# Sparse graph attention, layers 0 and 1: scores by accumulated transposes, one exponential per chunk, softmax sums as matmuls

## The chip, the cores and the metric

The kernel runs on one core of one Trainium2 chip. A core has TensorE (matmuls, with a weight load ahead of each), VectorE, ScalarE, GpSimd (called POOL in the profile, it issues the gathers here) and SyncE, which issues plain DMAs. Each takes its instructions in program order and waits on semaphores. The core also has 16 DMA engines. The metric is the device time of one execution in microseconds. Lower is better.

## The reference

Four graph layers follow one another on `x`, 8 batches of 2048 nodes of 128 features. One adjacency matrix, with about 16 neighbours per node, serves all. Layers 0 and 1 are attention with 8 heads of 16, restricted to neighbours, followed by a feed-forward network. Layers 2 and 3 are graph attention with one score per node pair.

```python
def layer01(adj_matrix, h, Wq, Wk, Wv, Wo, bo, ln1_g, ln1_b, W1, b1, W2, b2, ln2_g, ln2_b):
    Q, K, V = ((h @ w).reshape(B, N, NUM_HEADS, HEAD_DIM) for w in (Wq, Wk, Wv))
    scores = jnp.einsum('bnhd,bmhd->bhnm', Q, K) / jnp.sqrt(HEAD_DIM)
    scores = jnp.where((adj_matrix == 0)[None, None], -jnp.inf, scores)
    attn = jax.nn.softmax(scores, axis=-1)
    attn_out = jnp.einsum('bhnm,bmhd->bnhd', attn, V).reshape(B, N, OUT_DIM)
    x = _layer_norm(h + (attn_out @ Wo + bo), ln1_g, ln1_b)
    y = jax.nn.relu(x @ W1 + b1) @ W2 + b2
    return _layer_norm(x + y, ln2_g, ln2_b)

def layer23(x, adj, W, a_src, a_dst, ln_gamma, ln_beta):
    h = x @ W
    e = (h @ a_src)[:, :, None] + (h @ a_dst)[:, None, :]
    e = jnp.where(e >= 0, e, NEG_SLOPE * e)
    att = softmax(jnp.where(adj == 0, -jnp.inf, e))
    return _layer_norm(jnp.einsum('bij,bjd->bid', att, h) + x, ln_gamma, ln_beta)
```

## The kernel before

**Tiles and slots.** A start phase reads the adjacency matrix, makes a list of neighbours for every node and sorts the nodes by their number of neighbours. 16 tiles of 128 nodes follow, one node per partition. Tile t has `CAPS[t]` slots, from 30 down to 11; slot s of a tile holds the s-th neighbour of each of its 128 nodes. Unused slots get -1e30 in `lmask`, so their weight becomes 0. The first tile folds the neighbours beyond 28 of its 16 fullest nodes over all partitions (`folded`), with a query spread to match (`qf`) and a matrix `merge` that brings the parts together.

**Chunks.** In layers 0 and 1 a chunk is two slots (sometimes one), in layers 2 and 3 four. For each slot GpSimd issues an indirect DMA that gathers 128 rows of a table in DRAM: 2048 numbers per node in layers 0 and 1, keys and values of all 8 batches. There are six buffers `kv` for chunks; `fetch` (L1118) issues gathers up to four chunks ahead, as soon as a buffer's last reader is done.

**One attention chunk** (`attention_chunk`, L634) is a generator that the main loop steps on:

1. VectorE multiplies the keys in place by the query (L642, 2048 numbers per partition for two slots). The 128 products of a batch lie as 16 groups of 8 heads, so the sum within a head is a sum over the 16 groups.
2. VectorE folds the products, by halves and in place (L647): from 128 to 64 columns, and in chunks with `k // 2` even to 32 as well. TensorE adds up what is left with the identity matrix, 8 or 4 matmuls accumulating in the PSUM tile `pair` (L650).
3. ScalarE takes the exponential, one instruction per slot, since the mask is its bias per partition (L655), and writes `w` in SBUF.
4. Two chunks later VectorE multiplies the values by `w` in place (L661), and TensorE adds the slots up by transposing each of the 8 batches' 128 x 128 blocks into the accumulator `acc` (`add_up` and `turn_into`, L328), 8 transposes per slot.

After the last chunk of a tile `reciprocal_sums` (L461) adds the weights of all slots on VectorE in a tree (L469, L471), takes their min and max for a final test (L478, L479) and the reciprocal (L480). `scales` (L682) spreads it over the columns, turns it with TensorE and copies it out; `outputs` (L676) multiplies `acc` by it. Then a tail (`attention_tail`, two halves of four batches) computes projection, norms, feed-forward and the next layer's rows, mostly on TensorE and ScalarE.

**Order.** The schedule is written by hand. The loop in `layers` (L1189) goes over the chunks. For chunk i it does the second slot's add-up of chunk i-3, issues gathers, then step 1, a `slot()`, steps 2 and 3, a `slot()`, step 4 of chunk i-2 with its first slot's add-up, and a `slot()`. Each `slot()` steps on all running tails and threads by one stage, so that their instructions stand between those of the chunks on TensorE and ScalarE. At the end a flag says whether all sums were within `SUM_MIN` and `SUM_MAX`; if not, a general path (not taken here) computes everything again.

Of the kernel before, what the change touches and what calls it, by code (L numbers as in the profile page):

```python
# [8 lines left out]
F32 = mybir.dt.float32  # L9
F16 = mybir.dt.float16  # L10
BF16 = mybir.dt.bfloat16
# [38 lines left out]
SUM_MIN, SUM_MAX = 1e-25, 1e30  # L50
# [34 lines left out]
def sparse_path(ctx: ExitStack, tc: tile.TileContext, ins: dict, out: bass.AP, flag: bass.AP):  # L85
# [46 lines left out]
    )  # L132
    eps = const.tile([P, 1], F32, name="eps")
# [17 lines left out]
    lmask = const.tile([P, sum(CAPS)], F32, name="lmask")  # L151
# [309 lines left out]
    def reciprocal_sums(l, t, w, columns, folded):  # L461
# [3 lines left out]
        if l < 2:  # L465

            while n > 2:
                m = -(-n // 2)
                nc.vector.tensor_add(w[:, : n - m, :], w[:, : n - m, :], w[:, m:n, :])  # L469
                n = m  # L470
            nc.vector.tensor_add(sums, w[:, 0, :], w[:, 1, :])  # L471
        else:
            nc.vector.tensor_reduce(
                sums, w[:, :n, :].rearrange("p s c -> p c s"), axis=AX.X, op=ALU.add
            )
# [157 lines left out]

    def attention_chunk(l, c):  # L634
        box, t, k, ns = c["box"], c["t"], c["k"], c["ns"]
        if k == 0:
            box["acc"] = pacc.tile([P, NB, P], F32, tag="acc", name="acc")
            box["w"] = work.tile([P, max(CAPS), NB * NH], F32, tag="w", name="w")
        acc, w, q = box["acc"], box["w"], box["qf" if c["folded"] else "q"]
# [4 lines left out]
        width = D  # L644
        for _ in range(2 - k // 2 % 2):
            width //= 2
            nc.vector.tensor_add(kk[:, :, :, :width], kk[:, :, :, :width], kk[:, :, :, width : 2 * width])  # L647
        sc = pair[:, : ns * NB * NH].rearrange("p (s b h) -> p s b h", b=NB, h=NH)
        for j in range(0, width, NH):
            nc.tensor.matmul(  # L650
                sc, ident, kk[:, :, :, j : j + NH], start=j == 0, stop=j + NH == width
            )
        for i in range(ns):
            at = first[t] + k + i
            nc.scalar.activation(  # L655
                w[:, k + i, :], sc[:, i].rearrange("p b h -> p (b h)"), AF.Exp,
                bias=lmask[:, at : at + 1], scale=1.0,
            )
# [4 lines left out]
            w[:, k : k + ns, :].rearrange("p s (b h) -> p (s b) h", h=NH)[:, :, None, :]  # L663
# [3 lines left out]
        if c["folded"]:  # L667
            folded_sums(w[:, BASE:, :], box)
# [4 lines left out]
    def sums(l, t, box):  # L673
        box["r"] = reciprocal_sums(l, t, box["w"], NB * (NH if l < 2 else 1), box.get("folded"))
# [7 lines left out]
    def scales(l, box):  # L682

        box["scale"] = scale = work.tile([P, NB, P], F32, tag="oT", name="scale", bufs=1)
        if l < 2:
            r = box["r"].rearrange("p (b h) -> p b h", h=NH)
            nc.scalar.copy(
                scale.rearrange("p b (j h) -> p b j h", h=NH),
                r[:, :, None, :].to_broadcast([P, NB, HD, NH]),
# [127 lines left out]
    def gat_tail(l, t, box):  # L817
# [5 lines left out]
        else:  # L823
            n = work.tile([P, max(CAPS), NB * NH], F32, tag="w", name="n")
# [71 lines left out]
    def start():  # L896
# [54 lines left out]
        same = small.tile([P, NT, BINS], BF16, tag="same", name="same", bufs=1)  # L951
        more = small.tile([P, NT, BINS], BF16, tag="more", name="more", bufs=1)
# [26 lines left out]
        def neighbours(t):  # L979
            val = work.tile([P, max(CAPS), NB * NH], F32, tag="w", name="val")  # L980
# [207 lines left out]

    def layers():  # L1189
# [9 lines left out]
        for i in range(len(every) + 2):  # L1199
            c1, c, n1, n2 = (chunk(i + j) for j in range(-1, 3))  # L1200
            while added:
# [25 lines left out]
            if n1["l"] in (2, 3) and n1["folded"]:  # L1227
                go(n1)
            if c1["l"] in (2, 3) and c1["last"]:
# [8 lines left out]
            while weighed and len(weighed) > (2 if c["l"] in (0, 1) else 0):  # L1238
                c2 = weighed.pop(0)
                if c2["last"]:  # L1240
                    sums(c2["l"], c2["t"], c2["box"])
                    threads.append(scales(c2["l"], c2["box"]))
                go(c2, 2)
                added.append(c2)
# [536 lines left out]
```

## Time and profile before

| | us |
|---|---|
| median of 5 runs | 3145.77 (3118.6 to 3157.37) |
| the profiled execution | 3139.88, its span 3138.1 |
| first to last L642 (attention chunks) | from 170.7 to 2070.6 |
| layers 2 and 3 | from about 2080 to the end |

| group | count | busy us | mean ns |
|---|---|---|---|
| L642 VectorE, keys times query, 2048 per partition | 268 | 612.2 | 2284 |
| L328 TensorE, transposes into `acc` (all layers) | 8208 | 1089.4 | 287 |
| L650 TensorE, score matmuls, 128 columns | 3168 | 421.9 | 284 |
| L650 TensorE, the same, 64 columns | 176 | 21.3 | 272 |
| L503 ScalarE, 128 columns from PSUM | 512 | 146.5 | 377 |
| L496 ScalarE, 128 columns from PSUM | 512 | 181.4 | 367 |

A line of a group names the line of the kernel, the engine, the operation, output and inputs, their shapes and the count; then the busy time and the mean duration of one. Matmuls overlap, so the mean of one is longer than its share of the busy time: for L328 1089.4 us over 8208 is 133 ns. A matmul of fp32 numbers is two instructions, a transpose one. Behind a second bar stands the time that the engine sat idle just before the group, and who ended it.

### The profile page before, as it was taken

What the parts mean: (1) busy time and instruction counts of PE and PEld (TensorE: products, weight loads), DVE (VectorE), ACT (ScalarE), POOL (GpSimd) and SP (SyncE); (2) the same over time, 40 slices, a digit from 0 to 9 for tenths busy, and PEclk for the clock granted to TensorE, in tenths of its full rate; (3) what the DMA queues carried; (4) which work ended last, traced back from release to release, by engine and by line L of the source; (5) the groups of instructions that cost most, each with busy time, mean ns of one, the idle gap of its engine ahead of it and who ended that gap; (6) DMA issues with size and microseconds to landing.
All of it is one profiled execution on the core that took longest, in us unless ns stands there. A gap on an engine that the chain in (4) does not pass through costs nothing.

```text
span 3138.1 us, 52148 instructions
## 1 busy us (share of the span) xinstructions
PE 2575.6 (82%) x19258; PEld 2346.1 (75%) x19258; DVE 2748.6 (88%) x2960; ACT 1340.8 (43%) x4895; POOL 1787.9 (57%) x1296
## 2 busy tenths in 40 slices
PE   5766888888889996788898999996778888688786
PEld 4655777777888886677787888885677778577776
DVE  8898999999999997999999999985878876677886
ACT  3511344444445551243443545553445545144354
POOL 0266678588566534555456555544666654666662
PEclk8978999999999998999999999998888889888898
DMA  8688888898889867688888888866898987999994
GB/s 328 247 331 317 313 302 315 327 335 324 322 332 338 322 268 302 248 325 331 313 315 334 340 318 330 316 225 245 337 345 329 361 331 281 338 340 364 369 366 163
DMA packets 200692, 987.63 MB, mean 315 GB/s; under 512 B 31918, under 2 KB 33712, under 8 KB 128436
## 3 DMA queue, kind: packets, MB, share of 16 engines
q0 software_dynamic: 175024, 890.45, 76.0%
q1 hardware_dynamic: 20502, 75.52, 6.4%
q10 hardware_dynamic: 4904, 18.24, 1.5%
q8 instruction: 155, 2.54, 0.3%
q14 instruction: 107, 0.88, 0.1%
HBM read 937.16 MB, written 91.55 MB: 328 GB/s over the span
## 4 chain that ended last, share of the span: by engine, by line
PE 42%; DVE 28%; issue 11%; DMA 7%; ACT 6%; POOL 2%; another core or an unknown queue 1%; DVEq 0%; POOLq 0%; ACTq 0%
PE acc L328 17%; DVE kv L642 10%; DVE kv L661 9%; DMA kv<-table,lists 5%; PE pair L650 5%; DVE kv L647 4%; PE m L754 2%; PE m L733 2%; PE m L335 2%; PE m L328 2%; PE m L838 2%; PE m L550 2%; ACT n L846 2%; PE m L559 1%; DMA kv<-table,sorted_lists 1%
## 5 line engine op out<-in xcount | busy, mean ns | idle before, releaser
L321 POOL DMA_INDIRECT kv<-table,lists x955 | 1327.7, 1390 | 874.0 <-PE acc L328 550.5
L328 PE MATMUL acc<-ident,kv 128*128 128x128 f32 x8208 | 1089.4, 287 | 203.4 <-DVE kv L661 99.4
L328 PEld LDWEIGHTS acc<-ident,kv 128*128 128x128 f32 x8208 | 987.3, 149 | 303.3 <-issue 166.5
L642 DVE TENSOR_TENSOR kv<-kv,q 128x2048 f32<-128x2048 f32 (+1 forms) x282 | 629.3, 2231 | 51.6 <-DMA kv<-table,sorted_lists 18.5
L661 DVE TENSOR_TENSOR kv<-kv,w 128x2048 f32<-128x2048 f32 (+1 forms) x284 | 632.7, 2228 | 0.0
L650 PE MATMUL pair<-kv,ident 128*128 128x128 f32 (+1 forms) x3344 | 443.3, 283 | 151.1 <-DVE kv L647 64.9
L650 PEld LDWEIGHTS pair<-kv,ident 128*128 128x128 f32 x3344 | 410.8, 197 | 175.9 <-issue 102.4
L799 DVE TENSOR_TENSOR kv<-kv,pair 128x3584 f32<-128x3584 f32 (+1 forms) x150 | 540.1, 3601 | 2.2 <-PE acc L328 0.4
L655 ACT ACTIVATE w<-pair,lmask 128x64 f32<-128x64 f32 x554 | 144.8, 311 | 748.9 <-PE pair L650 720.2
L647 DVE TENSOR_TENSOR kv<-kv 128x1024 f32<-128x1024 f32 (+1 forms) x434 | 442.7, 1020 | 14.4
L496 ACT ACTIVATE n<-m,eps 128x128 f32<-128x128 f32 x512 | 181.4, 367 | 298.1 <-PE m L720 153.8
L321 POOL DMA_INDIRECT kv<-table,sorted_lists x153 | 182.7, 1194 | 142.8 <-PE acc L328 74.0
L846 ACT ACTIVATE n<-m,eps 128x128 f32<-128x128 f32 x256 | 90.7, 372 | 313.1 <-PE acc L328 133.8
L804 ACT ACTIVATE kv<-kv,ws 128x128 f32<-128x128 f32 x554 | 176.5, 402 | 92.8 <-DVE ws L793 51.3
L517 POOL DMA_INDIRECT table<-rows,perm x57 | 90.8, 1593 | 137.1 <-ACT score L570 39.9
L754 PE MATMUL m<-w_L_w,hT 128*128 128x128 f32 x1024 | 156.2, 275 | 0.0
L503 ACT ACTIVATE n<-m,rs 128x128 f32<-128x128 f32 x512 | 146.5, 377 | 1.1
L810 DVE TENSOR_TENSOR kv<-kv 128x1024 f32<-128x1024 f32 x75 | 91.5, 1221 | 62.1 <-ACT kv L804 62.0
L680 DVE TENSOR_TENSOR o<-acc,scale 128x512 f32<-128x512 f32 x128 | 82.7, 684 | 63.9 <-PE acc L328 33.2
L754 PEld LDWEIGHTS m<-w_L_w,hT 128*128 128x128 f32 x1024 | 134.9, 192 | 0.0
L733 PE MATMUL m<-n1T,w_L_gnn_W 128*128 128x512 f32 x256 | 131.5, 597 | 0.6 <-ACT q L608 0.6
L335 PE MATMUL m<-ident,n 128*128 128x128 f32 x640 | 110.2, 293 | 17.0 <-ACT n L854 8.0
(238 smaller groups left out, 3624.2 us busy)
## 6 DMA issues: line engine op xcount, KB each, us to landing
kept<-xT SPq DMA_DIRECT2D x48, 512.0 KB
xT<-kept SPq DMA_DIRECT2D x48, 512.0 KB
kv<-in_adj_dram SPq DMA_DIRECT2D x16, 1024.0 KB
table<-kv ACTq DMA_DIRECT2D x16, 1024.0 KB
kv<-table,lists POOLq DMA_INDIRECT x955
kv<-in_x_nodes_dram SPq DMA_DIRECT2D x16, 512.0 KB
kv<-table,sorted_lists POOLq DMA_INDIRECT x153
found<-cand POOLq DMA_DIRECT2D x16, 64.0 KB
```

Of the source, the lines that this page charges most:

```text
L321: nc.gpsimd.indirect_dma_start(out=dst, out_offset=None, in_=tables[l][:, :], in_offset=bass.IndirectOffsetOnAxis(ap=index, axis=0), bound ...
L328: nc.tensor.matmul(dst, src, ident, start=start, stop=True, is_transpose=True, skip_group_check=True)
L335: nc.tensor.transpose(pt[:, j * P : (j + 1) * P], src[:, j, :], ident)
L496: nc.scalar.activation(dst[:, i, :], z[:, i, :], AF.Square, bias=eps, scale=D**-0.5, accum_out=ss[:, i : i + 1],)
L642: nc.vector.tensor_mul(kk, kk, q[:, None].to_broadcast([P, ns, NB, D]))
L647: nc.vector.tensor_add(kk[:, :, :, :width], kk[:, :, :, :width], kk[:, :, :, width : 2 * width])
L650: nc.tensor.matmul(sc, ident, kk[:, :, :, j : j + NH], start=j == 0, stop=j + NH == width)
L661: nc.vector.tensor_mul(vv, vv, w[:, k : k + ns, :].rearrange("p s (b h) -> p (s b) h", h=NH)[:, :, None, :] .to_broadcast([P, ns * NB, HD, ...
L733: nc.tensor.matmul(ph, wt["1"][:, f * P : (f + 1) * P], n1T.rearrange("p b c -> p (b c)"), start=True, stop=True,)
L754: nc.tensor.matmul(y[:, j, :], hT[:, f, j, :], wt["2"][:, f, :], start=False, stop=f == 1, skip_group_check=True,)
L799: nc.vector.tensor_mul(hv[:, :, :nv, :], hv[:, :, :nv, :], wc[:, :, :nv, None].to_broadcast([P, ns, nv, D]))
L804: nc.scalar.mul(hv[:, i, b, :], hv[:, i, b, :], ws[:, i, b - nv : b - nv + 1])
```

## The change

Only layers 0 and 1 are touched. Gathers, the product of keys and query, the values' product, add-ups and tails stay.

- **Fold.** VectorE does one fold in every chunk (128 to 64 columns), and writes it to a new tile `hk`, ordered by group of heads j, then slot, batch and head.
- **Scores.** TensorE transposes the eight blocks `hk[:, j, :]`, adding them up in `pair[:m, :128]`. The scores now have slot, batch and head on the partitions, and the nodes along the columns. The mask can't be a bias any more: one bfloat16 matmul per slot adds it (`lmask` is now bfloat16). One exponential covers the chunk; it writes `eT`.
- **Turn back.** One chunk later TensorE transposes `eT` into `pair[:, 128:128 + m]`, and ScalarE copies that to `weights` in SBUF, which the values' product reads.
- **Sums.** After eight chunks, and after a tile's last chunk, matmuls of every `eT` with `fold_slots` (two identities of 64 on top of each other) add the weights up in PSUM. ScalarE copies the sum out, and after the last chunk takes its logarithm; `scales` uses exp(-log). The tree and the reciprocal are no longer run in layers 0 and 1; the min and max are. The bounds of the final test are narrower.
- **Order.** `scales` starts with the turn back of a tile's last chunk, some two chunks earlier. Every iteration of the main loop begins with the turn back of the chunk before.
- Tiles that shared the buffers of the old `w` get the new shape, and two tiles of the start phase use the buffers of `hk`.

```diff
-SUM_MIN, SUM_MAX = 1e-25, 1e30
+SUM_MIN, SUM_MAX = 1e-15, 1e15
...
+    fold_slots = const.tile([P, NB * NH], F32, name="fold_slots")
+    nc.vector.tensor_add(fold_slots, ident[:, : NB * NH], ident[:, NB * NH :])
...
-    lmask = const.tile([P, sum(CAPS)], F32, name="lmask")
+    lmask = const.tile([P, sum(CAPS)], BF16, name="lmask")
...
+    def block_sums(l, t, box, last):
+
+        terms = [(e, fold_slots[: e.shape[0], :]) for e, folded in box["exps"] if not folded]
+        if "partial" in box:
+            terms.append((ident, box["partial"]))
+        if last and t == 0:
+            terms += [(merge, box["wf"][:, i, :]) for i in range(FOLD)]
+        ps = misc()[:, : NB * NH]
+        for i, (a, b) in enumerate(terms):
+            nc.tensor.matmul(
+                ps, a, b, start=i == 0, stop=i + 1 == len(terms), skip_group_check=True
+            )
+        name = "sums" if last else "partial"
+        box[name] = small.tile([P, NB * NH], F32, tag=name, name=name)
+        nc.scalar.copy(box[name], ps)
+        box["exps"].clear()
+        if last:
+            box["r"] = small.tile([P, NB * NH], F32, tag="logs", name="logs", bufs=1)
+            nc.scalar.activation(box["r"], ps, AF.Ln)
+            threads.append(scales(l, box))
...
-        width = D
-        for _ in range(2 - k // 2 % 2):
-            width //= 2
-            nc.vector.tensor_add(kk[:, :, :, :width], kk[:, :, :, :width], kk[:, :, :, width : 2 * width])
-        sc = pair[:, : ns * NB * NH].rearrange("p (s b h) -> p s b h", b=NB, h=NH)
-        for j in range(0, width, NH):
+        m, at = ns * NB * NH, first[t] + k
+        hk = work.tile([P, NH, P], F32, tag="hk", name="hk")[:, :, :m]
+        kj = kk.rearrange("p s b (j h) -> p (s b) j h", h=NH)
+        nc.vector.tensor_add(
+            hk.rearrange("p j (c h) -> p c j h", h=NH), kj[:, :, :NH, :], kj[:, :, NH:, :]
+        )
+        sc = pair[:m, :P]
+        for j in range(NH):
+            turn_into(sc, hk[:, j, :], j == 0)
+        for i in range(ns):
             nc.tensor.matmul(
-                sc, ident, kk[:, :, :, j : j + NH], start=j == 0, stop=j + NH == width
-            )
-        for i in range(ns):
-            at = first[t] + k + i
-            nc.scalar.activation(
-                w[:, k + i, :], sc[:, i].rearrange("p b h -> p (b h)"), AF.Exp,
-                bias=lmask[:, at : at + 1], scale=1.0,
-            )
+                sc[i * NB * NH : (i + 1) * NB * NH, :],
+                lmask[:, at + i : at + i + 1].to_broadcast([P, NB * NH]), ident_bf,
+                start=False, stop=True, skip_group_check=True,
+            )
+        eT = box["eT"][:m, len(box["exps"]) % NH, :]
+        nc.scalar.activation(eT, sc, AF.Exp)
+        box["exps"].append((eT, c["folded"]))
+        yield
+        back = pair[:, P : P + m]
+        nc.tensor.matmul(
+            back, eT, ident[:m, :m], start=True, stop=True, is_transpose=True, skip_group_check=True
+        )
+        w = small.tile([P, P], F32, tag="weights", name="weights", bufs=3)[:, :m]
+        nc.scalar.copy(w, back)
...
+        if c["last"] or len(box["exps"]) == NH:
+            block_sums(l, t, box, c["last"])
         yield
...
-            nc.scalar.copy(
+            nc.scalar.activation(
                 scale.rearrange("p b (j h) -> p b j h", h=NH),
-                r[:, :, None, :].to_broadcast([P, NB, HD, NH]),
+                r[:, :, None, :].to_broadcast([P, NB, HD, NH]), AF.Exp, scale=-1.0,
             )
...
+            for c2 in weighed[-1:]:
+                go(c2)
             while added:
...
```

## The prediction

> **What bounds the kernel now.** I read the page's totals and slices first, to find the engine that is hardly ever idle in the attention layers, then the stages, the chain of waits in one of them, 10 us windows inside a tile, and the groups by shape.
>
> ```profile
> PE 2575.6 (82%) x19258; PEld 2346.1 (75%) x19258; DVE 2748.6 (88%) x2960; ACT 1340.8 (43%) x4895; POOL 1787.9 (57%) x1296
> ...
> DVE  8898999999999997999999999985878876677886
> ...
> DMA  8688888898889867688888888866898987999994
> ```
>
> Columns 3 to 26 are the two attention layers: VectorE shows 9 nearly throughout, DMA 8 and TensorE 6 to 9. The stages in numbers (span, TensorE, weight loads, VectorE, ScalarE, GpSimd, clock, DMA share, GB/s):
>
> ```profile
> 240.00:1045.00 805.00, 680.28 (x5256) 621.89 (x5255) 777.26 (x713) 342.22 (x1170) 562.96 (x328) 0.98 0.87 323
> 1250.00:2010.00 760.00, 670.90 (x5362) 618.72 (x5361) 733.94 (x544) 327.50 (x1241) 422.59 (x238) 0.98 0.84 316
> ```
>
> VectorE is idle for 28 us of 805 and 26 of 760. But TensorE has only 125 and 89 us to spare, and the DMA engines 13 to 16%. Two windows of 10 us inside one tile show that the three take turns:
>
> ```profile
> 1600.00:1610.00 10.00, 5.94 (x47) 5.31 (x48) 9.96 (x8) 2.00 (x6) 5.92 (x4) 1.00 1.02 427
> 1630.00:1640.00 10.00, 10.00 (x78) 8.87 (x77) 9.89 (x7) 6.15 (x21) 4.51 (x2) 1.00 0.72 261
> ```
>
> In the first no tail of an earlier tile runs: DMA is full, TensorE 60% busy. In the second a tail runs: TensorE never stops, DMA falls to 0.72. VectorE is full in both. The chain of waits of the first stage, by line, says who decides:
>
> ```profile
> by line: DVE kv L642 17.1%; DVE kv L661 16.0%; issue 9.7%; DMA kv<-table,lists 9.4%; PE acc L328 8.9%; DVE kv L647 7.5%; PE pair L650 6.5%; PE m L754 3.1%; PE m L733 3.1%; PE m L535 2.3%; DVE o L680 1.7%; PE m L335 1.7%; POOL kv L321 1.6%;
> ```
>
> Only 7.5% of the chain is the line that the change shortens. Summed by engine from its pieces, the chain is 47% VectorE and 31% TensorE here, 45% and 41% in layer 1. So VectorE is first, with TensorE and DMA close behind it.
>
> **VectorE: what goes.** The groups by shape:
>
> ```profile
> L661 DVE TENSOR_TENSOR kv<-kv,w 128x2048 f32<-128x2048 f32 x270 | 616.5, 2283 | 0.0
> L647 DVE TENSOR_TENSOR kv<-kv 128x1024 f32<-128x1024 f32 x270 | 330.5, 1224 | 8.8
> L647 DVE TENSOR_TENSOR kv<-kv 128x512 f32<-128x512 f32 x158 | 109.6, 694 | 5.4
> L655 ACT ACTIVATE w<-pair,lmask 128x64 f32<-128x64 f32 x554 | 144.8, 311 | 748.9 <-PE pair L650 720.2 <-issue 20.1 <-PE m L335 7.4
> ```
>
> There are 284 attention chunks, 270 of two slots and 14 of one. Of the 158 adds of 512 elements, 14 are first folds of one-slot chunks, so 144 are second folds; with six of 256 elements at some 0.42 us that is 144 x 0.694 + 2.5 = 102 us. The weight sums are L469 50.9 us (its sum over windows), L471 7.2 and the 64-wide reciprocal 17.7: 76 us. Together 178 us leave VectorE. The min and max of the sums stay. The first fold stays too, but it now writes `hk` in runs of 8 elements 128 apart. No row has such a write; L661 reads its weights in runs of 8 at 2.283 us, no more than L642's 2.284 with long runs, so I keep 1.224 us and add nothing. The other end, a write at half rate, is 284 x 1.22 = 346 us.
>
> **TensorE: exchanged.** L650 goes: 3344 instructions, two per matmul, 443 us busy, 0.133 each. In come 8 x 284 = 2272 transposes of one instruction each, like L328's (1089.4 us / 8208 = 0.133): 302 us. 284 transposes back: 38. For the sums, 302 matmuls of two instructions on 64 columns; L650's one-slot form on 64 columns took 1.90 us for 16 in a dense stretch, as the 128-column one (1.95), so again 0.133: 80 us. The 554 mask matmuls in bfloat16 have no row. Below lies half a bfloat16 weight load (L530: 101 ns), 28 us in all; above L961's 64-column bfloat16 matmul, 213 ns, 118 us; I take 0.11 each, a dense transpose's pitch, to which it is nearest: 61 us. Sum 481 against 443: 38 us more (5 to 95).
>
> **ScalarE** loses 145 us of exponentials on 64 columns. It gains 270 on 128 at L496's 0.367 and 14 at 0.31 (103 us), 284 copies at L503's 0.377 (107) and, for the sums, 80 instructions of 64 columns at 0.311 (25): 90 us more. It works 343 of 805 us now, so the work itself is covered by its idle time. Turning r into scale is one instruction of the same size as before. DMA issues, their order and GpSimd's queue are as before; the gathers are released by the same last add-up of a chunk.
>
> **The new waits.** Per chunk TensorE now waits twice for ScalarE. The turn back waits for the exponential; between it and the scores TensorE has eight add-ups (1.04 us in the timeline) that mostly wait for VectorE anyway, so I cost that at nothing; uncovered it would be 0.37 us plus the handover. And the next chunk's scores wait for the copy, because both lie in `pair`. Queued behind them are all add-ups and tails, and behind the add-ups the buffers that POOL gathers into. The copy is late where a tail's four squares and two roots (903.34 to 905.32 us in the timeline: 2.0 us) stand ahead of it: 2.0 + 0.37 against 1.04 of add-ups, 1.3 us exposed. Four such groups per tile, one in three falling in that place: 32 x 4/3 x 1.3 = 55 us on TensorE.
>
> **The sum.** Frozen chain: of L647's 117 us on it in the two stages (7.5% of 805, 7.4% of 760) 23% are second folds, 27 us; L469 has 26 there (its pieces), with L471 and L480 in proportion 39; 3 more between the layers. That is 69. TensorE has some 36% of the chain, so of its 38 + 55 us 33 come back: a gain of 36. At the other end VectorE stays the bound with today's idle share: stage 0 is 777 - 77 = 700 busy, 725 long; stage 1 734 - 73 = 661, 685 long: a gain of 155. But stage 0's other floors are just as high: TensorE 680 + 16 = 696, DMA 0.87 x 805 = 700; stage 1's TensorE is 671 + 16 = 687. Three resources that tie don't all run at 97%; I take 70, in the lower half, nearer the chain. The profiled execution took 3139.88 us (span 3138.1), 0.2% under the median of 3145.77, so I carry the gain over unchanged: 3140 - 70 = 3070.
>
> **Clock.** Transposes replace matmuls, so I looked for what transposes alone do to the granted clock:
>
> ```profile
> 2846.57 9.77 PE L328 MATMUL acc<-ident,kv 128*128 128x128 f32 x88
> ```
>
> 88 in a row at 0.111 us, and both 5 us windows inside read 1.00. Slow ones follow idle time: after 3.82 us idle, 16 of L650 took 3.75 us at 1723.05. The Trainium skill, "TensorE: Matmul & The Clock Gate", Part 4 (PE-mode transpose), says that full clock does not engage for transposes, since they don't count as TensorE activity; by it the change would lower the clock, to the time of rival 4. This trace disagrees: 1.00 in both windows.
>
> **Rivals.**
> 1. *Relief in full* (0.13): VectorE keeps today's idle share, gain 120 to 155, 2985 to 3020. For it: the kv buffers let DMA run three chunks ahead and even out its 0.72 and 1.02. Against: the equal floors above.
> 2. *No change* (0.16): the frozen chain with the masks at their upper price, another 57 x 36% = 20 off the 36, 3125; to 3170 where the copy waits double.
> 3. *Slower: TensorE waits out ScalarE on every chunk* (0.15). Exponential 0.37, copy 0.37, handover around 0.1 each: 0.94 us x 284 = 267 us, plus 38 of work. The idle 214 us in the two stages take up what they can, 91 remain: 3230. It decides once the exposed wait exceeds (214 - 38)/284 = 0.6 us per chunk. For it: ScalarE already sat 720 us waiting for L650, in step with TensorE. Against: in that time it had nothing queued, so it answers at once.
> 4. *Slow clock* (0.02): the nine transposes per chunk at 0.198 us, as 17 in 3.36 us at 2326.86, instead of 0.111: 0.78 x 284 = 222 us, 3290. The clock row above speaks against it. Or *strided writes* (0.02): 3140 + 346 - 178 = 3308.
>
> The forecast itself (3020 to 3110) has 0.52. Measurement tells about 1% from no change: 31 us, so faster means under 3114, slower over 3177. Faster: 0.52 + 0.13, with 0.01 lost at the edge, 0.64; same 0.17; slower 0.19. The range leaves out some 0.07 below and 0.13 above: 3000 to 3200.
>
> **What would show it.** Right: VectorE's busy time down by some 175 us in the attention layers; the fold at about 1.22 us; TensorE's score transposes in batches of eight at 0.9 to 1.1 us; VectorE idle up from 26 to some 60 us per stage, its releaser DMA or TensorE; DMA share 0.90 or more; clock not under 0.97. Wrong: a fold of 2 us; hundreds of us of TensorE idle before the scores or the turn back put down to ScalarE; TensorE busy over 720 us in a stage. The layers after 2160 us should not move.

## The result, and the profile after

The changed kernel takes 3128.11 us (median of 48 runs, 3105.81 to 3150.82) against 3141.09 (90 runs, 3117.35 to 3163.43) for the kernel before, measured along with it: a ratio of 0.9957 [0.9946, 0.9969], some 13 us faster. That is a real gain, but less than 1%. The profiled execution has a span of 3122.6 us, 15.5 less than before; the last product of keys and query of layer 1 starts at 2047.6 us instead of 2070.6, 23 earlier. Both differences are small beside the 157 us that VectorE was relieved of in the attention layers (195 to 2160 us: 1834.46 busy, now 1676.99). TensorE went the other way there, from 1690.13 to 1758.81.

The totals and two rows of slices of the changed kernel's page:

```profile
PE 2640.2 (85%) x19620; PEld 2356.4 (75%) x19620; DVE 2579.2 (83%) x2633; ACT 1348.0 (43%) x4989; POOL 1769.6 (57%) x1296
...
DVE  8888989988989877989888989865778876678886
...
DMA  8688888888999877788888888867998997899994
```

VectorE's row has lost most of its nines in columns 3 to 26. It is idle more often now, and the time hardly got shorter. The two stages by windows (columns as before: span, TensorE, weight loads, VectorE, ScalarE, GpSimd, clock, DMA share, GB/s):

```profile
240.00:1045.00 805.00, 724.38 (x5527) 641.68 (x5526) 719.57 (x585) 353.41 (x1235) 552.08 (x330) 0.96 0.88 327
1250.00:2010.00 760.00, 707.98 (x5588) 634.49 (x5586) 665.40 (x406) 336.05 (x1307) 409.33 (x239) 0.96 0.86 320
```

VectorE's idle time is 85 us of 805 and 95 of 760 (before: 28 and 26). TensorE has 44 us more work in the first stage, 37 in the second, and 81 and 52 us left. DMA moved 0.88 and 0.86 instead of 0.87 and 0.84: the gathers were hardly sped up. The chain of waits of the second stage, by line, before and after (the view breaks the lines off at their end; for the first stage it has no piece of the changed kernel's chain):

```profile
by line: DVE kv L642 16.6%; DVE kv L661 16.5%; PE acc L328 10.3%; PE pair L650 7.8%; issue 7.7%; DVE kv L647 7.4%; PE m L733 4.6%; PE m L754 4.2%; DMA kv<-table,lists 3.7%; PE m L603 2.4%; PE m L749 2.1%; PE m L335 2.0%; DVE w L469 1.9%; PE
```

```profile
by line: PE acc L330 17.6%; DMA kv<-table,lists 8.8%; PE pair L330 8.3%; issue 7.1%; DVE kv L692 6.3%; DVE kv L658 6.0%; PE m L766 5.6%; PE m L787 5.4%; PE m L337 3.3%; PE m L597 2.9%; PE m L637 2.8%; POOL kv L323 2.7%; PE m L782 2.7%; PE m
```

The two large products that headed it, 33.1% together, are down to 12.3% (L658, L692), and the fold is not in the part shown. Summed by engine from its pieces, 65% of this chain is TensorE (41% before), 15% VectorE (45% before), 9% DMA. So VectorE's part of the end went to TensorE. Groups by shape show what TensorE does now:

```profile
L663 DVE TENSOR_TENSOR hk<-kv 128x1024 f32<-128x1024 f32 x270 | 330.8, 1225 | 27.4 <-DVE kv L658 0.9 <-PE acc L330 0.5
L330 PE MATMUL pair<-ident,hk 128*128 128x128 f32 x2160 | 295.0, 282 | 115.5 <-DVE hk L663 107.9 <-ACT rs L481 2.8 <-ACT weights L684 1.6
...
L680 PE MATMUL pair<-ident,eT 128*128 128x128 f32 x270 | 76.2, 282 | 0.8 <-ACT eT L676 0.8
...
L676 ACT ACTIVATE eT<-pair 128x128 f32<-128x128 f32 x270 | 74.7, 277 | 441.2 <-PE pair L670 418.4 <-PE pair L330 15.9 <-issue 5.8
...
L684 ACT COPY weights<-pair 128x128 f32<-128x128 f32 x270 | 71.4, 264 | 384.1 <-PE pair L680 337.9 <-PE m L753 10.2 <-issue 8.4
L670 PE MATMUL pair<-ident_bf,lmask 128*64 128x128 bf16 x554 | 71.0, 247 | 0.0
...
L637 PE MATMUL m<-fold_slots,eT 128*128 128x64 f32 x536 | 68.2, 278 | 0.0
...
L670 PEld LDWEIGHTS <-lmask 128*64 128x64 bf16 x554 | 31.1, 106 | 50.5 <-issue 50.5
```

(The last columns are: busy time, mean ns of one, then the engine's idle time just before the group and what ended it.) The fold with its scattered write takes 1.225 us, as the old one. The score transposes and their 64-row form of the one-slot chunks, 14.5 us, make 309.5 us where L650 had 443. Turn back, masks and sums are new: 80.0, 71.0 and 75.4 us with their small forms. That is 536 against 443, 93 more by groups; but a single instruction's length overlaps with its neighbours, and in the windows, where overlapping instructions count once, it is 69. Before the masks' weight loads there stand 50.5 us of idle time that no wait explains. Counted by weight loads the exchange is 252.0 and 12.3 us for the scores, 41.7 for the turn back, 75.2 for the sums and 31.1 + 50.5 for the masks, 463 in all, where L650's took 411: 52 more. These are the loads of the scores, before and after:

```profile
L650 PEld LDWEIGHTS pair<-kv,ident 128*128 128x128 f32 x3344 | 410.8, 197 | 175.9 <-issue 102.4 <-DVE kv L647 47.2 <-ACT rs L487 15.2
L330 PEld LDWEIGHTS pair<-ident,hk 128*128 128x128 f32 x2160 | 252.0, 146 | 135.6 <-issue 105.2 <-ACT rs L481 8.9 <-DVE hk L663 7.7
```

So TensorE's added work is some 50 to 70 us, by either count.

One chunk in the timeline (start, length, engine and group; in brackets the idle time ahead):

```profile
902.70 1.01 PEld L330 LDWEIGHTS pair<-ident,hk 128*128 128x128 f32 x8
902.91 1.04 PE L330 MATMUL pair<-ident,hk 128*128 128x128 f32 x8
903.88 0.11 PEld L670 LDWEIGHTS <-lmask 128*64 128x64 bf16 x2 [0.17 <-issue]
903.88 0.25 PE L670 MATMUL pair<-ident_bf,lmask 128*64 128x128 bf16 x2
...
904.05 0.42 PEld L330 LDWEIGHTS m<-ident,scale 128*128 128x128 f32 x4
```

The eight score transposes keep the pitch of a row of them, 1.04 us. Then the two mask loads start 0.17 us after the last transposing load ended at 903.71, and the next group's load starts at 904.05: 0.34 us for two matmuls, where 0.22 had been forecast. It is the same in other chunks: in 224 places where the load behind the masks waited for nothing, the median is 0.34, which makes some 97 us for all masks (an estimate, 284 times 0.34). The standing isn't to be added to the masks' 71.0 us of busy time: it lies under the end of the transposes, which TensorE finishes at 903.95. The waits that VectorE sees, with those of TensorE's scores for the copy (us in all, count, longest):

```profile
DVE kv L658 <- DMA kv<-table,lists: 107.8, 72, 7.4
...
DVE kv L692 <- ACT weights L684: 28.4, 21, 3.6
...
DVE kv L658 <- DMA kv<-table,sorted_lists: 22.4, 6, 11.4
...
PE pair L330 <- ACT weights L684: 1.6, 5, 0.4
```

VectorE waits 130 us for gathers before L658 (108 + 22), where it was 42 before. TensorE's scores wait only 1.6 us for the copy of the weights.

### The profile page after: what moved, and what is told of

The parts are those of the page before. It is cut to its first block, busy times and chain, and to the rows that moved or that the text cites. A ratio compares the mean times of both kernels' runs of the same rounds, so it can differ in the third digit from the quotient of the medians.

```text
span 3122.6 us, 53258 instructions
## 1 busy us (share of the span) xinstructions
PE 2640.2 (85%) x19620; PEld 2356.4 (75%) x19620; DVE 2579.2 (83%) x2633; ACT 1348.0 (43%) x4989; POOL 1769.6 (57%) x1296
## 4 chain that ended last, share of the span: by engine, by line
PE 34%; issue 8%; DVE 6%; DMA 6%; ACT 4%; POOL 2%; another core or an unknown queue 1%; POOLq 0%; DVEq 0%; ACTq 0%
PE acc L330 15%; DMA kv<-table,lists 3%; POOL kv L323 2%; PE pair L330 2%; DMA kv<-table,sorted_lists 2%; DVE kv L658 2%; PE m L766 2%; PE m L787 2%; DVE kv L692 2%; PE m L330 2%; PE m L544 2%; PE m L553 2%; PE m L871 2%; PE m L337 1%; ACT n L879 1%
## 5 line engine op out<-in xcount | busy, mean ns | idle before, releaser
L330 PE MATMUL acc<-ident,kv 128*128 128x128 f32 x8208 | 1116.6, 288 | 173.8 <-issue 77.8
L330 PEld LDWEIGHTS acc<-ident,kv 128*128 128x128 f32 x8208 | 994.2, 150 | 258.5 <-issue 139.7
L658 DVE TENSOR_TENSOR kv<-kv,q 128x2048 f32<-128x2048 f32 (+1 forms) x282 | 630.1, 2234 | 153.7 <-DMA kv<-table,lists 100.4
L692 DVE TENSOR_TENSOR kv<-kv,weights 128x2048 f32<-128x2048 f32 (+1 forms) x284 | 633.9, 2232 | 30.6 <-ACT weights L684 28.4
L330 PE MATMUL pair<-ident,hk 128*128 128x128 f32 (+1 forms) x2272 | 309.5, 281 | 115.5 <-DVE hk L663 107.9
L330 PEld LDWEIGHTS pair<-ident,hk 128*128 128x128 f32 (+1 forms) x2272 | 264.3, 144 | 136.4 <-issue 105.8
L663 DVE TENSOR_TENSOR hk<-kv 128x1024 f32<-128x1024 f32 (+1 forms) x284 | 340.5, 1199 | 28.8 <-DVE kv L658 0.9
L676 ACT ACTIVATE eT<-pair 128x128 f32<-128x128 f32 (+1 forms) x284 | 78.5, 276 | 457.9 <-PE pair L670 434.9
L684 ACT COPY weights<-pair 128x128 f32<-128x128 f32 (+1 forms) x284 | 74.3, 262 | 392.1 <-PE pair L680 345.0
L511 POOL DMA_INDIRECT table<-rows,perm x57 | 83.7, 1468 | 136.2 <-ACT score L564 40.2
```

The costliest lines, as they stand in the source:

```text
L330: nc.tensor.matmul(dst, src, ident, start=start, stop=True, is_transpose=True, skip_group_check=True)
L658: nc.vector.tensor_mul(kk, kk, q[:, None].to_broadcast([P, ns, NB, D]))
L663: nc.vector.tensor_add(hk.rearrange("p j (c h) -> p c j h", h=NH), kj[:, :, :NH, :], kj[:, :, NH:, :])
L692: nc.vector.tensor_mul(vv, vv, w.rearrange("p (s b h) -> p (s b) h", b=NB, h=NH)[:, :, None, :] .to_broadcast([P, ns * NB, HD, NH]),)
```

## The experiments

Differences in us are the ratio's difference times the time of the kernel before, run beside it on the same chip (3019 to 3153 us). Where a kernel is compared with the changed one, that stands at 0.9957 as above, or at 0.9947 [0.9928, 0.9965] where it was run again.

A second measure comes from the traces: when the last product of keys and query of layer 1 starts (before: 2070.6 us). It leaves out the layers behind the attention, whose length differs between the measurements. Where one kernel has two traces, they agree in it within 5 us, though the whole executions differ by up to 144:

| kernel | last product of keys and query starts at, us |
|---|---|
| changed | 2047.6 and 2047.4 |
| before, VectorE relieved | 2031.8 and 2033.4 |
| before, TensorE relieved | 2039.3 and 2042.5 |
| before, both relieved | 1967.9 and 1963.5 |
| changed, sums on VectorE | 2021.0 |
| changed, no masks | 2014.1 |
| changed, turn back later | 2086.5 |
| changed, half of the score transposes | 2008.7 |
| changed, no turn back | 2030.4 |
| mask on ScalarE, sums on VectorE | 2003.9 and 2004.2 |
| the last, with a shorter hold | 2119.8 |

The kernels are explained below. There is one trace of the kernel before.

**Is VectorE's relief worth anything by itself?** The kernel before, without its second folds and without the tree of the sums: some 148 us less for VectorE (2748.6 busy on the page of before, 2600.5 on this one's), nothing new for any engine. The scores keep their 4 or 8 matmuls, and where the second fold is gone they miss half the products; the sums take two slots only.

```diff
-        width = D
-        for _ in range(2 - k // 2 % 2):
-            width //= 2
-            nc.vector.tensor_add(kk[:, :, :, :width], kk[:, :, :, :width], kk[:, :, :, width : 2 * width])
+        nc.vector.tensor_add(kk[:, :, :, : D // 2], kk[:, :, :, : D // 2], kk[:, :, :, D // 2 :])
+        width = D // 2 if k // 2 % 2 else D // 4
...
-            while n > 2:
-                m = -(-n // 2)
-                nc.vector.tensor_add(w[:, : n - m, :], w[:, : n - m, :], w[:, m:n, :])
-                n = m
```

> The kernel before with VectorE relieved and nothing added: the second folds and the tree of sums are left out (half of the products of every second chunk is not added up, and only the first two weights of a tile are summed, so scores and sums lack parts), while TensorE does its 4 or 8 score matmuls as before. VectorE loses about 102 + 51 us. Theory A (TensorE gave the relief back: TensorE is busy 69 us more in the attention stages of the changed kernel): the relief by itself is worth what was forecast, 60 us or more, ratio to before 0.981 or less. Theory B (TensorE and the gathers tied with VectorE from the start, so that the relief is worth little with or without the added work): at most 30 us, ratio 0.990 to 0.997.

Measured: 0.9853 [0.9831, 0.9876], 2979.10 against 3019.28: 44 us, 0.30 us per us taken away, which lies between the two theories. By the table the attention layers end 37 to 39 us earlier. The chain's own share of the same work was some 56 us (27 for the second folds, 26 for L469, 3 between the layers). So the relief is real, and alone, with no work added anywhere, it brings about a third of its size. What VectorE no longer does it waits for: 125 us before this kernel's keys product stand for gathers (105.4 and 19.7), where it was 42.

**What do the sums cost on TensorE?** The changed kernel with the sums on VectorE: one add of 128 columns per chunk, then one of 64, and the reciprocal, as before. With the reciprocal the start of `scales` goes back to where it was, so this run tests both together. (The diff shows the main lines.)

```diff
+        if k == 0:
+            box["added"] = small.tile([P, P], F32, tag="partial", name="added")
+            nc.vector.tensor_copy(box["added"], w)
+        elif not c["folded"]:
+            nc.vector.tensor_add(box["added"][:, :m], box["added"][:, :m], w)
...
-        if c["last"] or len(box["exps"]) == NH:
-            block_sums(l, t, box, c["last"])
```

> The changed kernel with the sums of weights back on VectorE, as one add of 128 columns per chunk (some 0.3 us, 85 us in all) and a reciprocal: TensorE loses 302 matmuls (604 instructions, some 75 us busy), ScalarE some 80 small instructions. Theory A: TensorE now decides, and VectorE has 180 us idle in the two attention stages: 15 to 35 us faster than the changed kernel, ratio to before 0.985 to 0.991. Theory B: what one engine is relieved of counts no more than what the other gets: within 8 us of the changed kernel, ratio 0.993 to 0.999.

Measured: 0.9856 [0.9835, 0.9878], some 27 to 30 us faster than the changed kernel. VectorE's busy time rises to 761 and 702 us in the two stages, TensorE's falls to 717 and 691. VectorE waits 67 us for gathers here (49.2 and 18.1), half of the changed kernel's 130. Moving this work from VectorE to TensorE, with all that hangs on it, was a loss.

**What do the masks cost?** The changed kernel without the 554 mask matmuls, so that empty slots count as nodes.

```diff
-        for i in range(ns):
-            nc.tensor.matmul(
-                sc[i * NB * NH : (i + 1) * NB * NH, :],
-                lmask[:, at + i : at + i + 1].to_broadcast([P, NB * NH]), ident_bf,
-                start=False, stop=True, skip_group_check=True,
-            )
```

> The changed kernel without the 554 mask matmuls (unused slots keep a weight, so the result lacks the mask): TensorE loses 71 us of busy time and some 50 us in which its weight loads stood still before them. Theory A: 40 to 70 us faster than the changed kernel, ratio to before 0.974 to 0.983. Theory B: VectorE idles because gathers come late, and TensorE's load is not what delays them: under 20 us, ratio 0.989 or more.

Measured: 0.9815 [0.9788, 0.9842], about 40 us faster than the changed kernel, 0.4 us for each of the some 97 that the masks held TensorE up. Without masks the change would have gained 56 us, about what VectorE's relief gives by itself.

**Does the turn back release the buffers or its reader late?** The add-ups of a chunk before the turn back and the block sums of the next, instead of behind them.

```diff
-            for c2 in weighed[-1:]:
-                go(c2)
             while added:
                 c2 = added.pop(0)
                 go(c2)
                 if c2["last"]:
                     threads.append(tail(c2["l"], c2["t"], c2["box"]))
+            for c2 in weighed[-1:]:
+                go(c2)
```

> The changed kernel with each iteration's add-ups of a chunk's second slot ahead of the turn back and the block sums instead of behind them, same work. Theory C (the turn back and the sums delay the release of the kv buffers: GpSimd's gathers waited 207 us for the turn back, VectorE 130 us for gathers against 42 before): 15 us or more faster than the changed kernel, ratio to before 0.991 or less. Theory A: TensorE's order does not change its load: within 8 us, ratio 0.993 to 0.999; slower if the scores now wait for the copy that stands directly ahead of them.

Measured: 1.0084 [1.0058, 1.0110], some 40 us slower than the changed kernel. The earlier release does what it was thought to do, VectorE's wait for gathers falls from 130 us to 102 (81.9 and 19.9), but the order as a whole loses more elsewhere. Other waits of this kernel show where (us in all, count, longest):

```profile
PEld pair L330 <- ACT weights L684: 92.5, 147, 1.4
...
PE pair L330 <- ACT weights L684: 47.6, 134, 0.4
```

Now the scores stand right behind the turn back, so they and their weight loads wait for the copy out of the same tile `pair`: 92.5 us on the weight loads and 47.6 on the matmuls, which stand at the same places and are not to be added, where the changed kernel has 3.7 and 1.6. VectorE's wait for the weights rises from 28.4 to 66.7 us. This is the wait that the prediction priced at 55 us. It exists, but only in this order.

**How hard does TensorE bind after the change?** The changed kernel with four of its eight score transposes, so with half the products in the scores.

```diff
-        for j in range(NH):
+        for j in range(NH // 2):
             turn_into(sc, hk[:, j, :], j == 0)
```

> The changed kernel with four of the eight score transposes per chunk left out (half of each score is missing), all else the same: TensorE loses 1136 transposes, some 125 to 150 us of work; VectorE, ScalarE and the gathers keep theirs. Theory A (TensorE decides most of the stage, at some 0.6 us per us of its work, as without the masks): 75 to 95 us faster than the changed kernel, ratio to before 0.965 to 0.972. Theory B (TensorE is one of three, the gain ends where VectorE and the gathers tie again): 35 to 55 us, 0.978 to 0.985.

The changed kernel beside it, unaltered:

> The changed kernel itself, beside the others of this call. Both theories: ratio to before 0.994 to 0.998.

Measured: 0.9787 [0.9761, 0.9813] against 0.9947 [0.9928, 0.9965]: 48 us for 1136 transposes of 0.111 us, 126 us. That is 0.38 us per us of the work taken out. TensorE's busy time fell by less, from 2554.5 us on the page of the changed kernel beside it to 2480.9, and its clock in the stages went from 0.96 and 0.97 to 0.93 and 0.95.

**How hard did TensorE bind before?** The kernel before with half of its score matmuls (1672 fewer, 186 us at 0.111), alone, and together with the relief of VectorE above. Half the products are missing in the first, up to three quarters in the second.

```diff
+        half = width // 2
-        for j in range(0, width, NH):
+        for j in range(0, half, NH):
             nc.tensor.matmul(
-                sc, ident, kk[:, :, :, j : j + NH], start=j == 0, stop=j + NH == width
+                sc, ident, kk[:, :, :, j : j + NH], start=j == 0, stop=j + NH == half
             )
```

> The kernel before with half of its score matmuls left out (half of the products that are left after the folds is not added up), VectorE unchanged: TensorE loses 1672 instructions, 186 us at the dense pitch of 0.111. If VectorE was the bound, as the prediction read it (VectorE idle 28 us of 805, TensorE 125): under 20 us, ratio 0.994 or more. If TensorE already decided part of the stages (the chain gives it 31 and 41%, and the runs so far 0.38 to 0.44 us per us of TensorE work): 60 to 80 us, ratio 0.974 to 0.980.

> e1 and g1 together: VectorE without second folds and tree, TensorE with half of its score matmuls. If two engines that take turns were all that bound the kernel, more than the sum of e1 (44 us) and g1: ratio to before 0.955 or less. If the gathers tie as third: about the sum or less, 0.96 to 0.975, with the DMA share of the stages at 0.92 or more.

Measured: 0.9898 [0.9872, 0.9924] and 0.9658 [0.9641, 0.9676], 32 and 107 us. The first lies between its two theories. In the second the DMA share of the first stage is 0.91 and of the second 0.88, under the 0.92 that the tie with the gathers would have shown. VectorE alone had been measured on another chip, so all three were run side by side:

> The kernel of e1 again (second folds and tree left out, TensorE as before), now on the same chip as r2 and r3. Ratio to before as measured, 0.983 to 0.988; call its gain a.

> The kernel of g1 again (half of the score matmuls left out, VectorE as before). Ratio 0.985 to 0.992; call its gain b.

> The kernel of g2 again, with both reliefs. Theory A' (VectorE and TensorE take turns as the bound and cover each other: each relief is partly lost until the other is made too): gain more than a + b by 15 us or more, ratio 0.970 or less where a + b alone give some 0.975. Independent gains: a + b within 10 us. The gathers as third bound: less than a + b.

Measured: VectorE 0.9838 [0.9801, 0.9875], TensorE 0.9883 [0.9862, 0.9903], both 0.9646 [0.9613, 0.9678], or 51, 37 and 112 us. The sum of the two is 88; the excess of 24 us is uncertain by some 17 (the three half-widths, 0.37, 0.20 and 0.33% of 3153, taken as independent). By the table above the attention layers end 37 to 39, 28 to 31 and 103 to 107 us earlier, an excess of 33 to 42. So each relief is partly lost until the other is made, as theory A' has it; the gathers as a third bound would have given less than the sum. The first stage by windows, with VectorE relieved, TensorE relieved, and both:

```profile
240.00:1045.00 805.00, 708.14 (x5397) 650.86 (x5398) 734.02 (x616) 352.52 (x1211) 546.79 (x332) 0.96 0.87 327
```

```profile
240.00:1045.00 805.00, 651.77 (x4632) 585.31 (x4631) 786.09 (x719) 346.15 (x1192) 560.27 (x330) 0.92 0.88 324
```

```profile
240.00:1045.00 805.00, 686.56 (x4907) 618.74 (x4907) 758.20 (x634) 368.72 (x1276) 575.75 (x345) 0.92 0.91 341
```

With one relieved, the other works as densely as before or more so (TensorE 708 in the first row, VectorE 786 in the second), and DMA stays at 0.87 and 0.88. With both, DMA goes to 0.91 and 341 GB/s. So neither engine is a floor that hides the other: each has its share of the chain, and the time falls by part of what either is relieved of.

TensorE's relief is smaller than it looks. Its busy time on the page fell by 93 to 95 us (2575.6 to 2483.0 and 2480.2) and not by 186, and the granted clock went from 0.98 to 0.92. So 32 to 37 us are 0.2 per us of the work taken out, but 0.3 to 0.4 per us that TensorE was really less busy; in the changed kernel with half of the scores these are 0.38 and 0.65.

**Is the cost in the new waits for ScalarE?** The changed kernel without the turn back and the copy; the values are multiplied by a constant of 1/16 and the sums stay.

```diff
-        back = pair[:, P : P + m]
-        nc.tensor.matmul(
-            back, eT, ident[:m, :m], start=True, stop=True, is_transpose=True, skip_group_check=True
-        )
-        w = small.tile([P, P], F32, tag="weights", name="weights", bufs=3)[:, :m]
-        nc.scalar.copy(w, back)
+        w = even[:, :m]
```

> The changed kernel without the turn back and its copy: the values are multiplied by a constant instead of the weights (scores, exponentials and sums are still computed). TensorE loses 284 transposes (some 40 us of its weight-load time), ScalarE 284 copies, and nobody waits for either. Theory A (the work counts, at 0.4 us per us): 12 to 25 us faster than the changed kernel, ratio to before 0.986 to 0.991. Theory D (the two waits for ScalarE per chunk cost more than the work, as in the prediction's rival 3): 50 us or more, ratio 0.978 or less.

Measured: 0.9920 [0.9892, 0.9948], 8 to 12 us faster than the changed kernel, with some 9 us of uncertainty; by the table 17 us in the attention layers. The instruction, its copy and both waits together cost no more than some 20 us.

**A version that keeps the gain.** The sums stay on VectorE as above, and the mask goes into the copy on ScalarE, which has idle time: it multiplies each slot's 64 columns by 1 or 0 as it takes them out of PSUM. Nothing is left out.

```diff
-        nc.scalar.copy(w, back)
+        for i in range(ns):
+            h = slice(i * NB * NH, (i + 1) * NB * NH)
+            nc.scalar.mul(w[:, h], back[:, h], lmask[:, at + i : at + i + 1])
```

> Everything is computed: sums on VectorE as in e2, and no mask matmuls; ScalarE multiplies by 1 or 0 per node and slot while it copies the weights out, two instructions of 64 columns per chunk instead of one of 128. TensorE loses 554 mask and 302 sum matmuls. Theory A: the gains of e2 (30 us) and e3 (43 us) add up but for VectorE's 85 us more: ratio to before 0.972 to 0.980. Theory B: VectorE is back at the bound with e2's load, ratio 0.983 to 0.988.

> v1 again (sums on VectorE, mask multiplied in by ScalarE; everything is computed). Ratio 0.972 to 0.982 if its gain does not hang on the chip it ran on.

Measured: 0.9762 [0.9743, 0.9782] (2951.79 against 3021.38) and, measured again where the kernel before took 3153.24, 0.9775 [0.9748, 0.9801]: some 70 us faster than the kernel before, and 55 faster than the changed one. Its stages by windows:

```profile
240.00:1045.00 805.00, 698.79 (x5208) 630.92 (x5208) 769.10 (x751) 382.91 (x1361) 570.41 (x340) 0.95 0.90 334
1250.00:2010.00 760.00, 675.65 (x5318) 618.38 (x5319) 706.14 (x559) 373.81 (x1469) 402.21 (x242) 0.96 0.86 323
```

TensorE is 18 and 5 us above the kernel before, VectorE 8 and 28 below it in the same windows, and DMA at 0.90 and 0.86. ScalarE's 383 us of 805 are still far from a bound.

**Are the gathers late because a chunk's buffer is held too long?** In that version VectorE still waits 67 us for gathers before L658. So the last version with the values' product one chunk earlier and with gathers sent further ahead:

```diff
-            if len(weighed) > 2:
+            if len(weighed) > 1:
...
-            if now[1] - now[0] > (4 if now[1] >= KVB and every[now[1] - KVB]["l"] > 1 else 3):
+            if now[1] - now[0] > 4:
```

> v1 with the values' product one chunk earlier (one chunk waiting instead of two), so that a kv buffer comes free one chunk sooner and gathers are issued five chunks ahead instead of four. If late gathers bound what is left (VectorE waits 130 us for them in the changed kernel): 15 to 40 us faster than v1. If TensorE's queue does: VectorE now waits for weights that TensorE and ScalarE have only just made, same or slower than v1 by up to 30 us.

Measured: 1.0143 [1.0120, 1.0166], over 110 us slower than the version it was made from, which neither theory had foreseen. Its waits for gathers before L658 fell to 8.4 us, but VectorE now waits for weights that have only just been made:

```profile
DVE added L690 <- ACT weights L680: 188.9, 120, 4.8
```

So the chunk between exponential and product hides the turn back. The gathers did come in time, and it didn't pay. The run changes two things at once, so it doesn't show what gathers sent further ahead would bring by themselves.

## Why the prediction was wrong in size

It named 3070 us and a gain over 1%; the gain was 13 us. The direction was right, and 3128 lies in the range.

- **VectorE's relief: right.** Forecast 178 us, measured 157 by the windows and 169 by the page's totals. The fold is 1.225 us, so scattered runs of 8 elements cost nothing and the strided-write rival falls.
- **What the relief is worth: the step that failed first.** The prediction worked out 36 us from the frozen chain and 155 from VectorE's idle share, and then says "I take 70, in the lower half, nearer the chain". There was no row for that choice. Relief alone brings 44 to 51 us (37 to 39 in the attention layers), and the chain's share of that work was 56. So even the frozen chain was somewhat high, and nothing of the way to 155 was there. (In the 69, the 39 for the sums were scaled up; the chain's own pieces of L469, L471 and L480 make 31.) Two thirds of VectorE's freed time was not on the path. Of the 154 us that it is idle more on the page (2579.2 of 3122.6, before 2748.6 of 3138.1), 88 are longer waits for gathers before L658. GpSimd, which issues the gathers, waits about as long as it did: 894 us before the gathers by `lists` in all layers, of it 410 put down to TensorE's add-ups and 172 to the turn back, where it was 874 and 550 to the add-ups. So the gathers came hardly sooner, and VectorE only reached them earlier.
- **TensorE's added work: mis-sized, by the masks.** Forecast 38 us more, measured some 50 to 70 (52 by weight loads, 65 by the page's totals, 69 by the windows). By weight loads the turn back is 41.7 (forecast 38), the sums 75.2 (80), the scores 264 (302). The masks, forecast at 61 (28 to 118), hold TensorE up for some 97 us, since no term held the 0.17 us in which their loads stand; they cost 40 us of the time. The turn back's 80 us by group are no sign of a wrong price: a lone transpose has a length of 282 ns in the trace but takes 0.147 us of the weight loads, and it is worth only 8 to 17 us of the time. The Trainium skill, "TensorE: Matmul & The Clock Gate", Part 4, gives some 275 ns for a bfloat16 transpose in one kernel's context. The trace agrees for float32, 282 ns, but this is a length: in a row they follow one another at 111 ns, so the length is not the price.
- **The copy's wait, 55 us on TensorE: wrong.** 1.6 us on the matmuls and 3.7 on the weight loads. The add-ups between the copy and the next scores cover it; it appears when they don't. The exponential's wait, costed at nothing, was right (0.8 us before L680).
- **ScalarE covered: right**, though its extra work was 10 us and not 90, since the exponential on 128 columns takes 277 ns (the prediction took 0.367 us) and the copy 264 (0.377 us).
- **The signs.** Batches of eight came at 1.04 us. VectorE idle rose to 85 and 95, over the 60 named, with DMA as its main releaser. DMA share of 0.90 or more: wrong, 0.88 and 0.86. Clock not under 0.97: wrong by 0.01. TensorE over 720 us in a stage was named as a sign of error, and the first stage shows 724. The later layers took 8 us longer, from 1067.5 to 1075.0 us behind the last L658. In the seven traces of other kernels that were measured where the kernel before took over 3130 us they took 1061 to 1090, and none of these kernels touches those layers, so the 8 us need not come from the change.

With the measured sizes the prediction's own frozen chain would still have been too high: 69 us off, and 36% of 52 to 69 given back, is a gain of 44 to 50, where 13 to 16 were measured, and 23 in the attention layers. Prices from the runs come nearer. 178 us of VectorE at 0.3 are 53, and 52 to 69 us of TensorE at 0.4 are 21 to 28, which leaves an estimate of 25 to 32, where the attention layers became 23 us shorter. This is not a closed account: the parts don't add up exactly (the excess of 24 us above), TensorE's price is 0.38 or 0.65 by how its work is counted, and why the whole gains less than the attention layers stays open. What the runs show without any sum is that the masks alone cost 40 us, the sums on TensorE 27 to 30 and the turn back 8 to 12, against a relief of 44 to 51.

Of the rivals, the second (no change, 3125) came nearest in time. It had the masks at their upper price, and they were well above the forecast; but its sum also holds the copy's wait, which wasn't there, and the frozen chain's 69, which was too much, so its closeness is partly luck. Relief in full falls: relief alone brings 51 at most and not 120 to 155. TensorE waiting out ScalarE falls by the constant-weights kernel, which gains only 8 to 12 us, and by the waits themselves; the handover of around 0.1 us that it counted has no row, and from 300 to 600 us of the changed kernel's trace ScalarE's copy most often starts 0.04 us after TensorE's turn back ends. The slow clock falls too: 0.96 in both stages. Taking work out of TensorE went with a lower clock, whether it was half of the old matmuls (0.92) or half of the new transposes (0.93), and with both engines relieved it was 0.92 at 687 us of busy time, where the kernel before has 0.98 at 680. So neither the number of transposes nor TensorE's idle time explains these rows, and why 0.98 became 0.96 stays open.

Not tried: the turn back in a PSUM bank of its own, and one mask matmul for both slots.

## What to carry to other kernels

Where two engines and the DMA all stand at 84 to 97%, don't price a change by the distance to the next floor. The share of the chain of waits is nearer (56 us for a relief that brought 44 to 51), and a run that only leaves work out is better still (here 0.3 us per us on VectorE and 0.2, then 0.4 on TensorE). Work moved from the fullest engine to one that is nearly as full gives most of its gain back, and the third engine's idle time is the better place: the mask on ScalarE and the sums left on VectorE were worth 55 us. Price matmuls by the time that they hold up the next weight load, since the lengths of single ones overlap, and look for loads that stand with nothing to wait for.

## What the runs showed of the hardware

- The masks' weight loads stand 0.17 us with nothing to wait for behind the float32 transposes: 50.5 us over 284 chunks, 0.178 each. That they are bfloat16 doesn't explain it. Between 195 and 2160 us of the changed kernel's trace 111 bfloat16 loads of 128x128 come directly behind float32 transposes of L330, and none of them stands. The masks' loads are 64 columns wide, and of 13 float32 turn backs that use only 64 rows 11 stand the same 0.17 us (three of them by the view for ScalarE), while those of 128 rows mostly don't:

```profile
897.56 0.91 PEld L330 LDWEIGHTS acc<-ident,kv 128*128 128x128 f32 x8
898.63 0.14 PEld L680 LDWEIGHTS pair<-ident,eT 64*128 64x128 f32 x1 [0.17 <-issue]
...
900.90 0.85 PEld L330 LDWEIGHTS acc<-ident,kv 128*128 128x128 f32 x8
901.72 0.10 PEld L524 LDWEIGHTS <-ones_bf 128*128 128x128 bf16 x1
...
907.26 0.14 PEld L680 LDWEIGHTS pair<-ident,eT 128*128 128x128 f32 x1
```

So it goes with loads that fill half of the array. It isn't the size alone: the 64-column transposes of one-slot chunks follow full ones in 9 places without standing. No run separates the two further.

- The same changed kernel took 3128.11 us in one measurement and 3005.03 in another, and the kernel before went along (3141.09 and 3021.38). The attention layers don't differ: between 200 and 1240 us TensorE is busy 923 and 924 us, DMA 0.86 in both, and the last L658 starts at 2047.6 and 2047.4. The layers behind them do. Windows after 2060 us, first of the slower measurement, then of the faster:

```profile
2060.00:2400.00 340.00, 255.76 (x1753) 232.19 (x1751) 244.70 (x272) 141.25 (x542) 193.69 (x179) 0.82 0.83 302
2400.00:2700.00 300.00, 233.98 (x1708) 217.34 (x1708) 219.53 (x254) 143.76 (x579) 171.69 (x164) 0.86 0.88 327
```

```profile
2060.00:2400.00 340.00, 267.76 (x2040) 251.74 (x2039) 287.04 (x324) 168.96 (x659) 230.37 (x211) 0.89 0.93 356
2400.00:2700.00 300.00, 244.35 (x1978) 232.69 (x1977) 240.96 (x279) 149.45 (x601) 192.15 (x184) 0.92 0.92 360
```

In the same time DMA moved 302 and 327 GB/s in the one, 356 and 360 in the other, TensorE's granted clock was lower with it (0.82 and 0.86 against 0.89 and 0.92), and all engines did less. Which of the two came first, the runs don't tell. Nor is it shown that the chip makes the difference: the version with the mask on ScalarE took 2951.79 and 3090.98 us, both under the same chip number on record. The ratios agree all the same, 0.9957 and 0.9947.
